# Four score banks, gathers three turns apart and another start of the experts at a kernel's change of stage

## The chip, the cores and the metric

One core of one Trainium2 chip runs the whole program. The metric is device time in microseconds of one execution. Three runs of the kernel before took 1683.93, 1685.1 and 1688.63 us; the median is 1685.1 us.

## The reference, cut to what matters

Sixteen rows of 512 tokens, 128 features wide, pass through six residual blocks:

```python
x = x + 0.5 * ffn0(layernorm(x))      # 128 -> 64 features, each through a small relu net, -> 128
x = x + attn0(layernorm(x))           # 16 heads of 8, 4 key heads, rotary positions, causal softmax
x = x + 0.5 * ffn0(layernorm(x))
x = x + 0.5 * moe(layernorm(x))       # 8 experts, 128 -> 512 -> 128
x = x + attn1(layernorm(x))           # a gated linear recurrence along the tokens
x = x + 0.5 * moe(layernorm(x))

def moe(x):                           # each expert chooses its 128 best tokens of a row
    probs = softmax(einsum('ntd,ed->nte', x, gate_w))
    g, m = top_k(probs.transpose(0, 2, 1), 128)
    h = einsum('nekf,efd->nekd', gelu(einsum('nekd,edf->nekf', x[batch, m], w1)), w2)
    return zeros.at[batch, m].add(g[..., None] * h)
```

## The kernel before

**Two parts.** First the rows go one after another through the small network and the attention, several rows in flight at different steps. Then come the experts: 256 jobs (2 expert blocks, 16 rows, 8 experts), with the recurrence of the fifth block between the two. Line numbers are those of the kernel before.

**Turns.** PE, ACT, DVE and POOL get a hand-made order. The steps are Python generators, and one turn (`turn`, L1104) advances each by one `yield`: first `flush` (L259) issues the copies left over from the last turn (`later`), then come `urgent` ones and `sides`, in list order. What is issued first stands first in its engine's queue, and each queue is in order. `need` (L221) holds a step back while the turn's budget for an engine is used up, as long as `paced` is set. `hurry` is false in the attention part and set at L1164.

**The last row's attention.** Row b has four head groups r of four heads. `weights` (L657) takes one entry of `BANKS` (L591, 11 entries) in a turn: score products on PE (L669) into a PSUM bank, the exponential on ACT (L672) into the tile `pt`, and a causal mask on POOL (L674). These exponentials are the "numerators" of the change's title. The bank comes from the pool `stp` with two buffers (L111), so the products of one turn wait for the exponential two turns before. The pool `scp` (L110), also two buffers, holds the scores from which `maxima` (L597) takes the row maxima of the next row; during the last row (b = 15) there is no next row. After a head group, `outputs` (L680) multiplies `pt` with the values into `ps_av` (L692), ACT copies that to `oT` (L696), PE transposes it (`ps_oq`, L704), and DVE divides by the sums into `y` (L708, L709) and appends r to `st["out"]` (L715). When all four are there, `stage_out` (L718) transposes y (`yT`, L721), multiplies (`ps_o`, L724), and runs the row through the second small network (`kan`, L329) and the gate (`gated`, L738). The norms in these use two POOL steps (L293, L294) between DVE steps. While the last row's attention runs, row 14 is in `stage_out` and `kan`.

**Gathers.** `fetch` (L850) gathers an expert's 128 token rows from DRAM with an indirect DMA that POOL issues (`xg`, L859), up to 16 ahead of what is transposed. It starts once the first head group's queries are done with (`taken`), as xg takes their place.

**Experts.** `dispatch` (L868) transposes gathered rows in pairs (`ps_x`, L883) and copies them to `xin` (L885, on ACT or DVE). `experts` (L891) takes three turns to a job: `ps_h` (L935) and Gelu (L937); `ps_y` (L950) and its scaling (L953); and for half the jobs products with a selection matrix into `acc` (L968), for the others an accumulating indirect DMA (L982). `ps_h` uses the banks of `scp`, `ps_y` those of `stp`. `experts` begins with two POOL steps (L908, L910). `routing` (L752) finds the top tokens on DVE, for eight rows at a time; `gated` counts scored rows for it. A job's gathers need that token list (`routed`).

**The end of the attention part** (L1164 to L1174):

```python
hurry[0], paced[0] = True, False
while len(sts[B - 1]["out"]) < NR:
    turn()
sides.append(stage_out(B - 1, sts[B - 1]))
sides.append(recurrences())
main = experts()
```

`experts` appends `dispatch` to the side tasks when it is first advanced (L925).

Of the kernel before, what the change touches and what calls it, by code (L numbers as in the profile page):

```python
# [8 lines left out]
F32 = mybir.dt.float32  # L9
# [7 lines left out]
P = 128  # L17
S = 512
# [7 lines left out]
NR = 4  # L26
# [20 lines left out]
def tile_macaron(  # L47
# [10 lines left out]
    B = x_in.shape[0]  # L58
# [40 lines left out]
    with ExitStack() as ph:  # L99
# [10 lines left out]
        scp = ph.enter_context(tc.tile_pool(name="p1_sc", bufs=2, space=PSUM))  # L110
        stp = ph.enter_context(tc.tile_pool(name="p1_st", bufs=2, space=PSUM))  # L111
# [78 lines left out]
        def packed(b):  # L190
            return [QP[(NR * b + r) % NQP] for r in range(NR)], KP[b % NKP]
# [29 lines left out]
        def need(**work):  # L221
            while paced[0] and any(w > room[e] for e, w in work.items()):
                yield
            for e, w in work.items():
                room[e] -= w

        def take(**work):

            for e, w in work.items():
                room[e] -= w  # L230
# [10 lines left out]
        held, kan_held, kans, hurry = [0], [0], [2 * B], [False]  # L241

        def bank(shape, dtype, name, work=0.0):


            while held[0] == 2 or (paced[0] and work > room["pe"]):
                yield
            room["pe"] -= work
            held[0] += 1
            return mm.tile(shape, dtype, name=name, tag="mm")  # L250

        def freed():
            held[0] -= 1
# [5 lines left out]
        def flush():  # L259
            for emit in later:  # L260
                emit()
            later.clear()
# [319 lines left out]
        def stage_in(b, st):  # L582
            late = b in through
            yield from kan_in(b)
            for _ in range(LATE if late and b > 2 else 0):
# [5 lines left out]
        BANKS = [(3, (0,)), (3, (1,)), (3, (2,)), (3, (3,)), (2, (0,)), (2, (1,)), (2, (2,)), (2, (3,)),  # L591
                 (1, (0, 1)), (1, (2, 3)), (0, (0, 1, 2, 3))]

        def in_bank(ps, gs):
            return ps.rearrange("p (u w) -> p u w", w=S // len(gs))
# [61 lines left out]
        def weights(b, st):  # L657

            qp, kp = packed(b)
            st["pt"] = {}  # L660
            for r in range(NR):
                pt = ptp.tile([P, NG, 1280], F32, name="pt")
                st["pt"][r] = pt
                for c, gs in BANKS:
                    c = NT - 1 - c
                    n = S - c * P
                    v = in_bank(stp.tile([P, S], F32, name="ps_st"), gs)
                    for u, g in enumerate(gs):
                        nc.tensor.matmul(v[:, u, 0:n], lhsT=kp[ROWS, r, bass.ts(c, P)],  # L669
                                         rhs=qp[r][ROWS, g, c * P : S], start=True, stop=True)  # L670
                    o = pt[:, gs[0] : gs[0] + len(gs), OFF[c] : OFF[c] + n]
                    nc.scalar.activation(o, v[:, :, 0:n], AF.Exp, scale=HD ** -0.5)  # L672
                    dg = o[:, :, 0:P]
                    nc.gpsimd.affine_select(out=dg, in_=dg, compare_op=ALU.is_ge, fill=0.0, base=0,  # L674
                                            pattern=[[0, len(gs)], [1, P]], channel_multiplier=-1)
                    if c == NT - 1:
                        taken[0] = NR * b + r + 1
                    yield

        def outputs(b, st, r):  # L680

            pt, va, y = st["pt"].pop(r), st["va"], st["y"]
            yield
            po = avp.tile([P, S], F32, name="ps_av")
            for c in range(NT):
                if c == 1:
                    yield
                if c < 2:
                    yield from need(pe=1.0 if c == 0 else 1.4)
                n = S - c * P  # L690
                for g in range(NG):
                    nc.tensor.matmul(po[32 * g : 32 * g + 32, c * P : S], lhsT=va[:, c, r, :],  # L692
                                     rhs=pt[:, g, OFF[c] : OFF[c] + n], start=(c == 0), stop=(c == NT - 1))
                if c == NT - 1:
                    oT = w2p.tile([P, NT, P], F32, name="oT")
                    later.append(lambda: nc.scalar.copy(oT.rearrange("p c q -> p (c q)"), po))  # L696
                if c in (0, NT - 1):
                    yield
            take(act=0.6)
            yield  # L700
            yield
            pq = yield from bank([P, NT, NG, 32], F32, "ps_oq", 0.5)
            for c in range(NT):
                nc.tensor.transpose(pq[:, c, :, :].rearrange("p r w -> p (r w)"), oT[:, c, :], ident)  # L704
            rd = small.tile([P, NT, NG, 1], F32, name="rden")

            def divide():
                nc.vector.reciprocal(rd, pq[:, :, :, HD : HD + 1])  # L708
                nc.vector.tensor_mul(y[:, :, r, :, :], pq[:, :, :, 0:HD], rd.to_broadcast([P, NT, NG, HD]))  # L709

            later.append(divide)
            yield
            take(dve=0.55)
            freed()
            st["out"].append(r)  # L715
            yield
# [131 lines left out]
        begun, fetched, moved = [0], [0], [0]  # L848

        def fetch():  # L850


            for i, (k, b, e) in enumerate(order):
                g, n = b // GB, (b % GB) * E + e
                while (k, g) not in routed or i >= moved[0] + 2 * E or taken[0] < NR * (B - 1) + min(i // E, 1) + 1:
                    yield
                if i in (0, E):
                    xgs.append(qkp.tile([CAP, E, D], F32, name=f"xg{i}", tag=f"qp{final[i // E]}"))
                nc.gpsimd.indirect_dma_start(  # L859
                    out=xgs[i // E % 2][:, i % E, :], out_offset=None, in_=xnd[b],  # L860
                    in_offset=bass.IndirectOffsetOnAxis(ap=tokI[g][:, n : n + 1], axis=0),
                )
                fetched[0] += 1

                for _ in range(3 if fetched[0] > moved[0] + 4 else 1):
                    yield

        def dispatch():  # L868
            while taken[0] < NR * B:
                yield  # L870
            for i in range(0, len(order), 2):
                while i + 1 >= fetched[0] or i > begun[0] + AHEAD:
                    yield
                if i in (0, E):
                    xins.append(qkp.tile([D, E, CAP], F32, name=f"xin{i}", tag=f"qp{final[2 + i // E]}"))

                own = kans[0] == 0
                if own:
                    ps = kap.tile([D, 2, CAP], F32, name="ps_x", tag="ps_kg")
                else:  # L880
                    ps = yield from bank([D, 2, CAP], F32, "ps_x")
                for j in range(2):
                    nc.tensor.transpose(ps[:, j, :], xgs[i // E % 2][:, i % E + j, :], ident)  # L883
                copy = nc.vector.tensor_copy if i % 4 else nc.scalar.copy
                later.append(lambda copy=copy, i=i, ps=ps: copy(xins[i // E % 2][:, i % E : i % E + 2, :], ps))  # L885
                yield
                if not own:
                    freed()
                moved[0] += 2

        def experts():  # L891
# [30 lines left out]
                else:  # L922
                    nc.sync.dma_start(out=out[b], in_=sums.pop((k, b)))

            sides.append(dispatch())  # L925
            while begun[0] < len(order) or any(line):
                now = None
                if begun[0] < moved[0]:
                    i = begun[0]
                    now = order[i] + (i % 4,)  # L930
                    k, b, e, u = now
# [11 lines left out]
                if line[1]:  # L943
                    k, b, e, u = line[1]
# [9 lines left out]
                if prod[2]:  # L954
                    v = line[2][-1]
# [5 lines left out]
                if prod[3]:  # L961
                    k, b, e, u = line[3]
# [16 lines left out]
                if line[2] and not prod[2]:  # L979
                    k, b, e, u = line[2]  # L980
                    g, n = b // GB, (b % GB) * E + e
                    nc.gpsimd.indirect_dma_start(  # L982
                        out=sums[k, b], out_offset=bass.IndirectOffsetOnAxis(ap=tokI[g][:, n : n + 1], axis=0),
# [104 lines left out]
        def recurrences():  # L1088
            while scored[0] < B:
                yield  # L1090
            for pair in range(B // 2):
                while done[0] < 2 * pair + 2:
                    yield
                yield from recurrence(pair)
# [4 lines left out]
        sts = [dict() for _ in range(B)]  # L1099
        urgent = []  # L1100
        sides = []
        TURNS = NR * len(BANKS)

        def turn():  # L1104
            flush()
            urgent[:] = [g for g in urgent if step(g)]
            sides[:] = [g for g in sides if step(g)]
            refill()
# [53 lines left out]
            if b >= 0 and b + 2 < B:  # L1162
                finish(ins[b + 2])
        hurry[0], paced[0] = True, False  # L1164
        while len(sts[B - 1]["out"]) < NR:
            turn()
        sides.append(stage_out(B - 1, sts[B - 1]))
        sides.append(recurrences())
        main = experts()
        working = True  # L1170
        while working or sides:
# [58 lines left out]
```

## Time and profile before

| what | value |
|---|---|
| median of three runs | 1685.1 us |
| profiled execution, its own time | 1679.07 us |
| its span on the profile | 1677.3 us |
| PE / DVE / ACT / POOL busy | 94% / 67% / 60% / 61% of the span |
| first gather, first ps_x, first ps_h | 919.02, 962.2, 964.73 us |
| gathers | 256, median 969 ns on POOL |

All times in what follows are microseconds from the start of the span of this one execution; 1.8 us of its time lie outside the span. "Busy" counts an engine's instructions from start to end; a PE that runs at a lower granted clock is busy for longer with the same work. A row of the timeline gives start, duration, engine, line, operation, output and input, and in brackets the idle time just before it with what ended that. A row of the waits gives the waiting instruction, what it waited for, the total in us, how often, and the longest. A row of the table by stretches gives start and end, length, and for each engine its busy time and number of instructions, then PE's granted clock as a share of full rate, the share of the DMA engines in use and GB/s.

### The profile page before, as it was taken

Reading aid. Unit: us, or ns where it says so; the run is one execution under the profiler, and the core shown is the slowest. Engines: PE = TensorE matmul, PEld = TensorE weight load, DVE = VectorE, ACT = ScalarE, POOL = GpSimd, SP = SyncE. Lnnn points to the kernel's source line nnn. Section 1 sums busy time; section 2 is a strip of 40 time slices with the busy share of each in tenths; the row PEclk is TensorE's granted clock in tenths of the full one; section 3 lists DMA queues with packets and bytes.
Section 4 is the critical chain, followed back from the end, with each engine's and each line's share of the span. In section 5 each row is a group of like instructions: output and inputs, shape, how many; then the busy total and the mean of one; then the engine's idle time right before and its main releaser. Section 6 shows DMA issues by size and latency. Waiting matters only on the chain.

```text
span 1677.3 us, 35404 instructions
## 1 busy us (share of the span) xinstructions
PE 1573.0 (94%) x12943; PEld 1093.7 (65%) x12943; DVE 1124.6 (67%) x3606; ACT 1002.3 (60%) x2000; POOL 1023.6 (61%) x1486
## 2 busy tenths in 40 slices
PE   5689999999999999999999799999999999999998
PEld 2234444444444544455444399888998889999998
DVE  6578878888888888888986146843469544672222
ACT  3446677787777877777777565444443434444454
POOL 2635557556665556565634757657766668667774
PEclk9779999999999999999999799999999999999999
DMA  4210111111101110111122114223323233333333
GB/s 123 67 63 26 56 50 40 33 42 57 53 30 40 49 57 23 40 52 56 35 81 62 30 40 78 58 52 76 64 59 64 58 61 73 67 64 75 70 77 58
DMA packets 103093, 94.87 MB, mean 57 GB/s; under 512 B 13197, under 2 KB 91478, under 8 KB 102678
## 3 DMA queue, kind: packets, MB, share of 16 engines
q1 hardware_dynamic: 76060, 67.65, 13.1%
q0 software_dynamic: 26048, 24.93, 9.4%
q8 instruction: 102, 1.67, 0.4%
q14 instruction: 73, 0.60, 0.1%
q10 hardware_dynamic: 810, 0.02, 0.0%
HBM read 59.00 MB, written 37.49 MB: 58 GB/s over the span
## 4 chain that ended last, share of the span: by engine, by line
PE 71%; DVE 19%; ACT 5%; issue 3%; POOL 2%; DMA 1%; DVEq 0%; SPq 0%; POOLq 0%; ACTq 0%
PE ps_h L935 12%; PE ps_y L950 11%; PE ps_av L692 7%; PE ps_st L669 6%; PE ps_sc L611 5%; DVE below L616 5%; PE acc L968 4%; PE ps_kg L365 4%; PE ps_s L338 3%; PE ps_t L318 3%; DVE ln_st L287 2%; ACT pt L672 2%; PE ps_ko L386 2%; PE ps_h L1076 2%; PE ps_h L1075 1%
## 5 line engine op out<-in xcount | busy, mean ns | idle before, releaser
L674 POOL TENSOR_SCALAR_AFFINE_SELECT pt<-pt 128x128 f32<-128x128 f32 (+2 forms) x704 | 252.7, 366 | 331.4 <-ACT pt L672 326.6
L672 ACT ACTIVATE pt<-ps_st 128x512 f32<-128x512 f32 (+1 forms) x704 | 378.8, 563 | 99.8 <-PE ps_st L669 94.0
L616 DVE CUSTOM_DVE_ANT_0 below<-ps_sc,causal 128x512 bf16<-128x512 f32 (+1 forms) x512 | 315.0, 615 | 80.1 <-PE ps_sc L611 64.8
L937 ACT ACTIVATE mo<-ps_h 128x512 f32<-128x512 f32 x256 | 152.8, 597 | 290.4 <-PE ps_h L935 288.5
L859 POOL DMA_INDIRECT xg<-xnd,tokI x256 | 252.3, 986 | 80.9 <-issue 45.0
L669 PE MATMUL ps_st<-qp,kp 99*128 99x512 bf16 (+3 forms) x1024 | 258.5, 305 | 21.7 <-ACT pt L672 20.8
L935 PE MATMUL ps_h<-xin,mw 128*128 128x128 f32 x2048 | 278.3, 279 | 0.0
L950 PE MATMUL ps_y<-mw,mo 128*128 128x128 f32 x2048 | 271.1, 275 | 0.4 <-DVE mo L959 0.4
L611 PE MATMUL ps_sc<-kp,qp 72*128 72x512 bf16 (+3 forms) x1024 | 259.6, 305 | 11.6 <-DVE maxs L616 6.6
L935 PEld LDWEIGHTS ps_h<-xin,mw 128*128 128x128 f32 x2048 | 249.7, 192 | 6.1 <-issue 3.2
L950 PEld LDWEIGHTS ps_y<-mw,mo 128*128 128x128 f32 x2048 | 249.1, 192 | 1.5 <-DVE mo L959 1.3
L982 POOL DMA_INDIRECT sum<-ye,tokI x124 | 201.4, 1624 | 63.4 <-ACT ye L953 22.7
L669 PEld LDWEIGHTS <-kp 99*128 99x128 bf16 x1024 | 95.1, 100 | 181.7 <-issue 164.4
L371 ACT ACTIVATE kan_h<-kan_s,rbias,kw 128x512 f32<-128x512 f32 x256 | 205.7, 812 | 3.8 <-PE ps_kg L365 3.8
L692 PE MATMUL ps_av<-pt,va 128*32 128x512 f32 (+3 forms) x2048 | 165.5, 441 | 0.0
L621 DVE TENSOR_REDUCE maxs<-ps_sc 128x2 f32<-128x512 f32 (+1 forms) x192 | 130.1, 685 | 34.9 <-PE ps_sc L611 34.4
L611 PEld LDWEIGHTS <-qp 72*128 72x128 bf16 x1024 | 96.2, 99 | 79.8 <-issue 57.2
L956 DVE TENSOR_TENSOR mo<-mo 128x128 bf16<-128x128 f32 x132 | 38.2, 290 | 129.4 <-ACT mo L941 129.1
L692 PEld LDWEIGHTS ps_av<-pt,va 128*32 128x32 f32 x2048 | 53.7, 109 | 94.9 <-issue 44.1
L968 PE MATMUL acc<-mo 128*128 128x128 bf16 x1584 | 111.3, 219 | 3.1 <-DVE mo L956 3.0
L968 PEld LDWEIGHTS <-mo 128*128 128x128 bf16 x1584 | 98.6, 98 | 19.9 <-issue 18.6
L294 POOL TENSOR_TENSOR ln_rstd<-ln_rstd,mhalf 128x4 f32<-128x4 f32 x96 | 101.1, 1053 | 8.0
(197 smaller groups left out, 2362.2 us busy)
## 6 DMA issues: line engine op xcount, KB each, us to landing
qp<-qs SPq DMA_DIRECT2D x64, 288.0 KB
xnd<-kan_x SPq DMA_DIRECT2D x32, 256.0 KB
sum<-x SPq DMA_DIRECT2D x31, 256.0 KB
qs<-qpart SPq DMA_DIRECT2D x48, 128.0 KB
kp<-ks SPq DMA_DIRECT2D x48, 96.0 KB
x<-in_L_attn_x_dram SPq DMA_DIRECT2D x16, 256.0 KB
mw<-in_L_ffn_w_dram SPq DMA_DIRECT2D x16, 256.0 KB
xg<-xnd,tokI POOLq DMA_INDIRECT x256
```

The costliest lines, as they stand in the source:

```text
L371: nc.scalar.activation(h, sk[half], AF.Relu, bias=rbias[:, half, v : v + 1], scale=kw1[:, half, v : v + 1])
L611: nc.tensor.matmul(v[:, u, 0:n], lhsT=qp[r][0 : 9 * HD, g, bass.ts(c, P)], rhs=kp[0 : 9 * HD, r, 0:n], start=alone, stop=(u == len(gs) - 1 ...
L616: nc.vector.tensor_tensor_reduce(below[:, 0:n], v[:, 0, 0:n], causal[:, S - n : S], 1.0, LOWEST, ALU.add, ALU.max, accum_out=maxs[:, c, h ...
L669: nc.tensor.matmul(v[:, u, 0:n], lhsT=kp[ROWS, r, bass.ts(c, P)], rhs=qp[r][ROWS, g, c * P : S], start=True, stop=True)
L672: nc.scalar.activation(o, v[:, :, 0:n], AF.Exp, scale=HD ** -0.5)
L674: nc.gpsimd.affine_select(out=dg, in_=dg, compare_op=ALU.is_ge, fill=0.0, base=0, pattern=[[0, len(gs)], [1, P]], channel_multiplier=-1)
L692: nc.tensor.matmul(po[32 * g : 32 * g + 32, c * P : S], lhsT=va[:, c, r, :], rhs=pt[:, g, OFF[c] : OFF[c] + n], start=(c == 0), stop=(c == ...
L859: nc.gpsimd.indirect_dma_start(out=xgs[i // E % 2][:, i % E, :], out_offset=None, in_=xnd[b], in_offset=bass.IndirectOffsetOnAxis(ap=tokI[ ...
L935: nc.tensor.matmul(pst[:, f, :], lhsT=mw1[e][:, bass.ts(f, P)], rhs=xins[i // E % 2][:, i % E, :], start=True, stop=True)
L950: nc.tensor.matmul(py, lhsT=hs[u][:, f, :], rhs=mw2[e][:, f, :], start=(f == 0), stop=(f == NF - 1))
L968: nc.tensor.matmul(acc[:, c, :], lhsT=sels[u][:, bass.ts(c, P)], rhs=yes[u][:, w, :], start=(e == 0 and c == 0 and w == 0), stop=(e == las ...
L982: nc.gpsimd.indirect_dma_start(out=sums[k, b], out_offset=bass.IndirectOffsetOnAxis(ap=tokI[g][:, n : n + 1], axis=0), in_=ye[:, b % 2 * ( ...
```

## The change

It has four parts. In the last row, every second entry of `BANKS` (counted over the four head groups) takes its bank from `scp` instead of `stp`; the new tile is called `ps_sl`. `outputs` notes in `st["read"]` how many head groups have had their last product into ps_av issued. `fetch` waits three turns after a gather, unless `hurry` is set and fewer than five gathers are ahead; before, it waited one turn whenever fewer than five were ahead. At the end of the attention part `dispatch` joins the side tasks at once, ahead of `stage_out` of the last row and `recurrences`, and the loop ends when the last head group's products have been issued, rather than when its y has been.

```diff
@@ weights @@
-                for c, gs in BANKS:
+                for i, (c, gs) in enumerate(BANKS):
                     c = NT - 1 - c
                     n = S - c * P
-                    v = in_bank(stp.tile([P, S], F32, name="ps_st"), gs)
+
+                    if b == B - 1 and (r * len(BANKS) + i) % 2:
+                        ps = scp.tile([P, S], F32, name="ps_sl", tag="ps_sc")
+                    else:
+                        ps = stp.tile([P, S], F32, name="ps_st")
+                    v = in_bank(ps, gs)
@@ outputs @@
                 if c == NT - 1:
+                    st["read"] = r + 1
@@ fetch @@
-                for _ in range(3 if fetched[0] > moved[0] + 4 else 1):
+                for _ in range(1 if hurry[0] and fetched[0] <= moved[0] + 4 else 3):
                     yield
@@ experts @@
-            sides.append(dispatch())
             while begun[0] < len(order) or any(line):
@@ tile_macaron @@
         hurry[0], paced[0] = True, False
-        while len(sts[B - 1]["out"]) < NR:
-            turn()
+        sides.append(dispatch())
         sides.append(stage_out(B - 1, sts[B - 1]))
         sides.append(recurrences())
+        while sts[B - 1]["read"] < NR:
+            turn()
         main = experts()
```

## The prediction

> **What bounds the kernel now.** I read the page first: engine shares, the 40 slices, and the chain that ended last.
>
> ```profile
> PE 1573.0 (94%) x12943; PEld 1093.7 (65%) x12943; DVE 1124.6 (67%) x3606; ACT 1002.3 (60%) x2000; POOL 1023.6 (61%) x1486
> ...
> PE   5689999999999999999999799999999999999998
> ...
> PEclk9779999999999999999999799999999999999999
> ```
>
> TensorE is busy nearly throughout and carries 71% of the chain, so only time in which it idles or runs at a low clock can be won. After the first slices there is one such place: slice 23 of 40, from about 922 to 964 us, with a 7 in both rows. There the last row's attention ends and the experts begin, which is where the change works. I then cut that stretch where the output products (ps_av) of each head group of the last row begin, with the experts' steady part behind it.
>
> ```profile
> core 0: us, PE busy (x) PEld busy (x) DVE busy (x) ACT busy (x) POOL busy (x), PEclk, DMA share, GB/s
> ...
> 907.50:918.60 11.10, 9.54 (x90) 5.68 (x88) 5.40 (x22) 8.21 (x17) 5.44 (x14) 1.00 0.45 125
> 918.60:933.20 14.60, 10.13 (x67) 5.26 (x66) 3.13 (x13) 7.11 (x14) 12.95 (x22) 0.79 0.13 32
> 933.20:945.80 12.60, 10.10 (x63) 3.59 (x62) 0.55 (x2) 10.02 (x19) 8.33 (x15) 0.77 0.07 18
> 945.80:955.70 9.90, 8.69 (x67) 3.64 (x66) 0.55 (x2) 7.86 (x15) 5.99 (x15) 0.91 0.08 20
> 955.70:970.20 14.50, 11.68 (x101) 9.54 (x101) 6.83 (x28) 5.27 (x9) 7.77 (x12) 0.88 0.15 42
> 970.20:1677.30 707.10, 697.30 (x6553) 653.75 (x6551) 364.01 (x1206) 327.19 (x773) 480.46 (x430) 1.00 0.33 65
> ```
>
> Each stretch has another limit. In the first (918.6 to 933.2, "A") POOL is busy 12.95 of 14.60 us. In the second ("B") ACT is the fullest at full rate, 10.02 of 12.60; PE's 10.10 is at a clock of 0.77. In the third ("C") it is PE, 8.69 of 9.90. In the tail ("T") nothing is full. The timeline of A shows why POOL counts:
>
> ```profile
> 923.62 0.94 POOL L859 DMA_INDIRECT xg<-xnd,tokI  x1 [0.17 <-issue]
> ...
> 925.05 0.94 POOL L859 DMA_INDIRECT xg<-xnd,tokI  x1 [0.17 <-issue]
> 926.03 0.25 POOL L293 TENSOR_SCALAR ln_rstd<-ln_mv 128x4 f32<-128x4 f32 x1
> 926.36 1.05 POOL L294 TENSOR_TENSOR ln_rstd<-ln_rstd,mhalf 128x4 f32<-128x4 f32 x1
> ...
> 927.44 0.78 DVE L308 TENSOR_TENSOR kan_x<-x,ln_rstd 128x512 f32<-128x512 f32 x1 [6.18 <-POOL ln_rstd L294]
> ...
> 928.27 1.12 PE L318 MATMUL ps_t<-ident,kan_x 128*128 128x128 f32 x4 [3.48 <-DVE kan_x L308]
> ```
>
> Row 14's norm has its sums on DVE at 921.3, but its two POOL steps stand behind five gathers (919.02, 920.76, 922.20, 923.62, 925.05); PE waits 3.48 us in its queue for what follows. The waits of PE from 917 to 970 us name the rest:
>
> ```profile
> PE ps_st L669 <- ACT pt L672: 4.9, 9, 0.7
> PE ps_t L318 <- DVE kan_x L308: 3.5, 1, 3.5
> PE ps_t L318 <- DVE y L709: 1.9, 1, 1.9
> PE ps_oq L704 <- ACT oT L696: 0.7, 1, 0.7
> ```
>
> The first is the two-bank rotation, the last two belong to T.
>
> **The gathers.** Nothing is added: 256 gathers as before. In the built order of POOL, two of them now stand ahead of row 14's two norm steps, where five did. Each costs 0.94 plus about 0.17 of issue, so 3 x 1.11 = 3.3 us leave A. If POOL sets A, the wait for its last mask before the next ps_av (932.98) moves by that much. After it, POOL needs 4 gathers (4.5), 11 masks (8 x 0.30, 2 x 0.41, 0.64) and the norm (1.3): 9.6 us from 919.0, so A could shrink by at most 5.0. I take 3.4, as PE then reaches the transposition a little before its input still, and its clock is better. The gathers' cost does not vanish: 11 instead of 16 have been issued when the first transposition of gathered rows (ps_x) is queued. The missing five come later on POOL, which is busy 480 of 707 us in the experts; what hides them is that PE sets the pace there.
>
> **Four banks.** The rotation's 4.9 us in 9 waits are PE's, not the path's: behind a waiting score product on PE stand ps_av, the FFN products and the transpositions, and ACT waits for those in turn (the waits of ACT: oT 4.0 us, the exponentials pt 4.8 in all). No instruction is added: of the last row's 64 score products 32 (22 of its 44 banks) write a bank of the other pool, whose readers (the maxima) are finished by 908.4; its next users are the experts' ps_h, after the last of them. With four banks PE may be four turns ahead of ACT, so ACT has about 2 us of exponentials (0.60 each) queued while PE does a ps_av lump of 1.50. The floors are the fullest engine: B cannot be below 10.0 (gain at most 2.5), C not below 8.7 (at most 1.2). I take half of each, 1.3 and 0.6, because from 937.5 to 945.0 ACT runs without a break already. Row 15's first head group (907.5 to 918.6) has PE at 9.54 of 11.10 and depends on the same row-14 work; I count nothing there.
>
> Here a rule speaks against the change. Cut into pieces of 3.4 us, the granted clock falls to 0.50 in three spells (927.0 to 933.9, 940.7 to 947.5, 961.2 to 964.6). The one at 940.7 follows 3.4 us in which PE was 1.85 us busy and never waited over 0.8; spells with 2.84 of 3.40 or more busy stayed at 1.00. The Trainium skill ("TensorE: Matmul & The Clock Gate", section "A second HAM failure mode: psum-queue depth-cycling") says that a product loop which cycles through PSUM banks idles so finely that the clock swings between half and full; more banks to cycle would then change nothing, B and C would keep their length, and the sum would lose 1.9. By the row, what counts is the busy share. B would have about 8.2 us of full-rate products in 11.3, 73%, between the 54% that fell and the 84% that held. I take one cold spell left in the loop, mostly under ACT; that is why B gets half only.
>
> **Experts from "read".** In the built order, three ps_x pairs now stand between the last ps_av products, and the first two ps_h ahead of and behind ps_oq, instead of after the whole chain oT, ps_oq, y, ps_t. They fill PE's idle 0.70 (for oT), 1.87 (for y) and 0.25, and the half-rate spell from 961.2, in which 3.02 us busy were worth 1.5. T holds 11.68 - 1.5 = 10.2 us of full-rate work in 14.5, so at most 4.3. The Gelu table load (1.28 us on ACT) now comes before row 15's yT copy; PE has the second ps_h, ps_x and ps_t meanwhile, and without that cover it would cost its 1.3. I take 3.0. Moved with it: dispatch stands ahead of row 15's output stage among the side tasks and takes PSUM banks first, so row 15's scores come at expert job 20 instead of 18 (built order), its token list at job 51 instead of 49. DMAs keep their number; on SP two row stores swap places. PE's order from the k=1 jobs on is the same.
>
> **Sum.** A 3.4, B 1.3, C 0.6, T 3.0: 8.3 us off. The profiled execution (span 1677.3, its time 1679.07) would come to 1670.8; it lies 6.0 below the median of the runs, 1685.1, to which the same difference applies: 1676.8. All floors reached: 5.0 + 2.5 + 1.2 + 4.3 = 13.0, 1672.1.
>
> **Rivals.** *Cold loop* (25%): PE's clock still falls in A and B, and ACT and PE keep each other's pace. Then the gathers give 2.5 and T 1.5: 1681. For it: ACT is unbroken for 7.5 us of B. Against: the fall at 927 follows the 3.48 us wait that goes.
> *The banks do nothing, the rest works* (inside the forecast's range): 1685.1 - 6.4 = 1678.7.
> *Nothing arrives* (9%): row 14's chain is limited by ACT's own queue, and what T gains is waited for at the experts' first products: 1684.
> *Gathers become the bound* (6%, slower): with 11 instead of 16 ahead, and three turns to a gather as to an expert job, the lead stays smaller: 9 instead of 14 at the first pair, mostly 4 to 5 instead of 5 to 6 for jobs 50 to 120. Before, a pair's gathers end 8.1 to 16 us ahead of their ps_x there; the one wait (1.2 us) came where only 0.17 was left, 3.5 sufficed. One gather less takes about one job, 2.6 us. The pair of jobs 58 and 59 had 9.3 us and loses two jobs to the later token list: about 4.1 left. It decides only if POOL lags 3 us more: then some 30 pairs would each pay about 0.5, 15 us in all, against the 8.3: 1692.
>
> **How the numbers follow.** The forecast has 60%, the cold loop 25%, nothing 9%, slower gathers 6%. A measurement of this kernel tells about 0.3%, 5 us: faster is below 1680.0. Most of the forecast case and a small part of the cold loop lie there: 0.66. Within: 0.26. Slower, with small unseen losses beside the last rival: 0.08. The range runs from all floors (1672.0) over the cold loop, with 2.5 us of spread, to 1683.5.
>
> **What would show it.** Right: the norm's POOL steps near 922.7 and PE's wait for kan_x under 1 us; A about 11 us long; waits of PE for ACT on score products under 2 us in total; first ps_h about 948 to 950 on the span, before ps_oq; at most one spell at 0.50 in the loop; the experts from the fifth ps_h on shifted as a block. Wrong: ps_x waiting for DMA by more than a few us, a longer experts' part than 707 us, or B still 12.6 with PE at half clock.

## The result and the profile after

The changed kernel takes 1676.4 us (median of 5 runs, 1675.01 to 1678.27); the kernel before, timed with it, takes 1684.19 (5 runs, 1682.11 to 1688.63). The ratio is 0.9951, with a 95% interval of 0.9934 to 0.9968, so 5.4 to 11.1 us are gone. The forecast was 1676.8. Its sum, 8.3 us, meets the measured difference of 7.8; the terms of the sum do not all meet theirs, as follows.

The profiled execution after took 1675.11 us (span 1673.4). The first lines of its page answer to those shown of before:

```profile
PE 1578.0 (94%) x12943; PEld 1095.9 (65%) x12943; DVE 1123.0 (67%) x3606; ACT 1001.9 (60%) x2000; POOL 1023.5 (61%) x1486
...
PE   5689999999999999999999899999999999999998
...
PEclk9779989999999999999999999999999999999999
```

The number of instructions is the same on every engine. In slice 23 of 40 the 7 of the clock is now a 9, and the 7 of PE an 8. The same cuts as before, at the starts of the last row's ps_av groups, in the table by stretches:

```profile
914.40:924.60 10.20, 9.39 (x89) 5.57 (x86) 5.31 (x22) 7.55 (x17) 5.06 (x13) 1.00 0.48 136
924.60:933.80 9.20, 8.06 (x68) 4.15 (x68) 3.15 (x13) 6.66 (x14) 8.31 (x16) 1.00 0.09 21
933.80:945.00 11.20, 9.17 (x63) 3.28 (x62) 0.55 (x2) 10.05 (x20) 9.71 (x18) 1.00 0.09 26
945.00:954.30 9.30, 9.03 (x69) 3.82 (x68) 0.56 (x3) 8.08 (x16) 6.82 (x16) 1.00 0.11 29
954.30:967.00 12.70, 12.13 (x117) 10.13 (x117) 7.22 (x30) 7.16 (x14) 8.73 (x12) 1.00 0.20 53
967.00:1673.40 706.40, 696.37 (x6534) 651.97 (x6533) 362.25 (x1204) 325.53 (x768) 482.93 (x432) 1.00 0.33 65
```

A went from 14.6 to 9.2, and POOL's 12.95 in it to 8.31. The clock was 0.79, 0.77, 0.91 and 0.88 from A to T and is 1.00 in every row. T is shorter and nearly full: PE 12.13 of 12.70. How row 14's norm got on its way, from the timeline:

```profile
927.70 0.97 POOL L865 DMA_INDIRECT xg<-xnd,tokI  x1 [0.17 <-issue]
928.95 0.24 POOL L293 TENSOR_SCALAR ln_rstd<-ln_mv 128x4 f32<-128x4 f32 x1
...
930.36 0.78 DVE L308 TENSOR_TENSOR kan_x<-x,ln_rstd 128x512 f32<-128x512 f32 x1 [3.07 <-POOL ln_rstd L294]
931.19 0.66 PE L318 MATMUL ps_t<-ident,kan_x 128*128 128x128 f32 x4 [1.01 <-DVE kan_x L308]
```

DVE's wait for the norm's POOL steps fell from 6.18 to 3.07, PE's in turn from 3.48 to 1.01, and its transposition takes 0.66 us at full rate instead of 1.12. The waits of PE from 914 to 977 us:

```profile
PE ps_t L318 <- DVE y L715: 1.3, 2, 0.7
PE ps_t L318 <- DVE kan_x L308: 1.0, 1, 1.0
PE ps_sl L674 <- ACT pt L677: 0.7, 1, 0.7
...
PE ps_st L674 <- ACT pt L677: 0.6, 1, 0.6
```

The score products wait 1.3 us in 2 waits, where they waited 5.5 in 10 over the same part (from 907 us; 4.9 in 9 from 917).

**Reading two spans against each other.** The last row's first score product starts at 907.53 us before and at 914.45 after, 6.92 later, although no engine's order ahead of it has changed. PE's half-rate time ahead of that mark was 54.6 us before and 68.3 after. When each kernel was profiled again, the marks were at 910.63 (before) and 913.65 (after). So the spans differ by 3.9 us only, while the changed stretch itself, from that mark to the first ps_h of expert job 48, went from 186.51 to 175.48: 11.0 us less. From there the parts are alike, 255.20 and 255.35 to job 128, 328.11 in both from there to the end. In what follows I therefore compare lengths from that mark. The repeats show how well these stand: 186.57 for before and 175.50 for after.

### The profile page after: what moved, and what is told of

Same layout as the page of the kernel before. It is cut to its first block, busy times and chain, and to the rows that moved or that the text cites. A ratio compares the mean times of both kernels' runs of the same rounds, so it can differ in the third digit from the quotient of the medians.

```text
span 1673.4 us, 35410 instructions
## 1 busy us (share of the span) xinstructions
PE 1578.0 (94%) x12943; PEld 1095.9 (65%) x12943; DVE 1123.0 (67%) x3606; ACT 1001.9 (60%) x2000; POOL 1023.5 (61%) x1486
## 4 chain that ended last, share of the span: by engine, by line
PE 72%; DVE 18%; ACT 4%; issue 3%; POOL 3%; DMA 0%; DVEq 0%; POOLq 0%; ACTq 0%
PE ps_h L940 12%; PE ps_y L955 11%; PE ps_av L697 7%; PE ps_st L674 6%; PE ps_sc L611 6%; DVE below L616 5%; PE acc L973 5%; PE ps_kg L365 3%; PE ps_s L338 3%; PE ps_t L318 3%; ACT pt L677 2%; DVE ln_st L287 2%; PE ps_h L1081 2%; PE ps_ko L386 2%; PE ps_h L1080 1%
## 5 line engine op out<-in xcount | busy, mean ns | idle before, releaser
L677 ACT ACTIVATE pt<-ps_st 128x512 f32<-128x512 f32 x682 | 368.3, 563 | 97.1 <-PE ps_st L674 91.4
L674 PE MATMUL ps_st<-qp,kp 99*128 99x512 bf16 x992 | 251.8, 305 | 16.7 <-ACT pt L677 16.2
```

## The experiments

Each length in the table runs from the mark to the first ps_av group of the last head groups ("0"), then from group to group (A, B, C), and from the last group to job 4 (T). "Half rate" gives where, in us behind the mark, the granted clock was 0.50 up to job 48, and in brackets for how long.

```
kernel               gathers   0      A      B      C      T    mark to  half rate
                     ahead*                                      job 4
before                  5    11.04  14.64  12.60   9.93  16.53   64.74   19.5 (6.8) 33.2 (6.8) 53.7 (3.4)
after                   2    10.14   9.21  11.21   9.32  12.69   52.57   none
e1 banks only           5    10.14  14.15  11.22   9.91  16.62   62.04   20.3 (3.4) 51.1 (3.4)
e2 pace only            2    11.04   9.46  12.30   9.49  18.37   60.66   30.2 (3.4) 47.3 (6.8)
e3 start only           5    11.04  14.66  12.60  10.93  12.24   61.47   19.5 (6.8) 33.2 (6.8) 166.3 (13.7)
e4 gather every turn    5    11.05  14.65  14.02   9.23  15.78   64.73   19.5 (6.8) 33.2 (6.8) 74.2 (3.4)
e5 after, two banks     2    11.04   9.46  12.29   9.77  12.93   55.49   30.3 (3.4) 163.5 (10.2)
e6 after, old pace      5    10.14  14.62  12.59  10.12  12.24   59.71   19.6 (6.8) 33.3 (3.4) 70.8 (3.4) 166.4 (13.7)
e7 after, old start     2    10.26   9.22  11.21   9.10  17.71   57.50   47.3 (3.4)
e8 after, six turns     1    10.14   8.34  11.21   9.32  16.42   55.43   47.7 (3.4) 160.4 (13.7)
e9 after, more          1    10.14   8.37  10.96   9.07  12.70   51.24   none
e10 after again         2    10.14   9.22  11.21   9.32  12.70   52.59   none
e11 before again        5    11.04  14.64  12.63   9.95  16.54   64.80   19.6 (6.8) 33.2 (6.8) 53.7 (3.4)
e12 after, late dispatch 2   10.14   9.22  11.21   9.10  14.88   54.55   none
* gathers ahead of row 14's norm steps in POOL's built order
```

The measured medians (this kernel, before on the same chip, ratio with its 95% interval):

```
e1   1744.05  1743.21  0.9990 [0.9967, 1.0013]      e7   1726.76  1746.44  0.9911 [0.9881, 0.9940]
e2   1744.26  1743.21  0.9982 [0.9954, 1.0011]      e8   1738.36  1746.44  0.9967 [0.9949, 0.9985]
e3   1743.45  1743.21  0.9985 [0.9961, 1.0008]      e9   1669.75  1683.74  0.9909 [0.9886, 0.9932]
e4   1742.69  1743.21  1.0004 [0.9979, 1.0029]      e10  1674.46  1683.74  0.9936 [0.9912, 0.9960]
e5   1732.10  1746.44  0.9922 [0.9900, 0.9945]      e11  1681.81  1683.74  0.9990 [0.9972, 1.0007]
e6   1742.16  1746.44  0.9982 [0.9961, 1.0002]      e12  1672.46  1683.74  0.9934 [0.9907, 0.9960]
```

The runs of e1 to e4 were on one chip and those of e5 to e8 on another, on which the kernel before takes some 60 us more than in the first comparison and in that of e9 to e12. That time lies in the experts' part and is told at the end; up to the tail, the lengths of unchanged parts agree with those of the first comparison to 0.02 us, with one exception in e3. So for e1 to e8 the verdicts rest on the lengths of one profile each, and the ratio is a second witness only: the intervals of e1 to e4 and of e6 all hold 1.

My theory was that three separate gains add up: the gathers ahead of the norm set A, the banks set B and C, the early start sets T. The rivals were that the clock does it, and that one part does nothing.

**e1, the banks alone.**

```diff
-                for c, gs in BANKS:
+                for i, (c, gs) in enumerate(BANKS):
...
-                    v = in_bank(stp.tile([P, S], F32, name="ps_st"), gs)
+                    if b == B - 1 and (r * len(BANKS) + i) % 2:
+                        ps = scp.tile([P, S], F32, name="ps_sl", tag="ps_sc")
+                    else:
+                        ps = stp.tile([P, S], F32, name="ps_st")
+                    v = in_bank(ps, gs)
```

> The kernel before with the four banks alone. The stretch from the first score product of the last row to the first ps_h of expert job 48 took 186.5 us before and 175.5 after. Theory of separate causes: five gathers still stand ahead of row 14's norm on POOL, so A loses only the bank waits (about 1 us), B loses 1.4 and C 0.6, the tail nothing: stretch near 183.5, time about 3 us below before (ratio 0.998). Rival, the clock does it: the 3.5 us wait of PE in A stays, the clock falls behind it as before, and B and C keep their 12.6 and 9.9: stretch 186, ratio 1.000.

A and B of e1, from the table by stretches:

```profile
921.80:935.90 14.10, 9.41 (x67) 5.21 (x66) 3.16 (x13) 6.89 (x15) 12.63 (x21) 0.88 0.09 28
935.90:947.20 11.30, 9.27 (x67) 3.34 (x69) 0.55 (x2) 10.00 (x19) 8.21 (x16) 1.00 0.09 25
```

Banks take 0.9 us from the first head group and 1.4 from B. A stays at 14.15, with POOL at 12.63 of it: the banks leave A's cause where it was, and the 0.5 us that it lost belong to a shorter half-rate spell (see "Why the prediction was right"). C does not gain from banks alone (9.91).

**e2, the pace of the gathers alone.**

```diff
-                for _ in range(3 if fetched[0] > moved[0] + 4 else 1):
+                for _ in range(1 if hurry[0] and fetched[0] <= moved[0] + 4 else 3):
```

> The kernel before with the three-turn spacing of the gathers alone. Separate causes: two gathers instead of five stand ahead of the norm, A goes from 14.6 to about 11, B and C stay at 12.6 and 9.9 because two banks still tie PE to ACT, tail unchanged: stretch near 182.5, ratio 0.998. Rival, the clock does it: without the long wait no spell of 0.50 follows in A or B, and B and C shrink as they did after (11.2, 9.3) though the banks are two: stretch near 179.5, ratio 0.996.

A falls to 9.46 with two banks as well. B stays at 12.30, and nine score products still wait for ACT, 5.5 us in all. The tail gets longer, 18.37 against 16.53. The trace shows where a part of that comes from: two of the gathers that the new pace puts off (950.38 and 951.63) now stand ahead of the POOL steps of row 14's next norm (952.61), and DVE waits 2.30 us for these, against 1.50 before, where one gather stood there and POOL still waited for DVE. The last y, and PE's ps_t of it, stand behind this norm: ps_t starts 6.39 us behind the last group's first ps_av, before 5.59. Besides, the half-rate spell in the tail is 6.8 us long instead of 3.4.

**e3, the start alone.**

```diff
+                    st["read"] = r + 1
...
-            sides.append(dispatch())
...
-        while len(sts[B - 1]["out"]) < NR:
-            turn()
+        sides.append(dispatch())
         sides.append(stage_out(B - 1, sts[B - 1]))
         sides.append(recurrences())
+        while sts[B - 1]["read"] < NR:
+            turn()
```

> The kernel before with dispatch and the experts started early alone. Separate causes: A, B and C as before (14.6, 12.6, 9.9), only the tail gains, 2.6 us by job 48: stretch near 184, ratio 0.9985. Rival: the tail's gain in the changed kernel came only because PE arrived there at full rate; then the stretch is 186 and the spell of 0.50 behind 961 stays.

T falls by 4.3, and C rises by 1.0. Of this, 0.3 is the first pair of gathered rows, whose transposition now stands in C (958.23), and 0.8 a longer wait of a score product for ACT (1.32 us, before 0.55), for which the edit gives no reason. Net 3.3.

**e4, the opposite of the new pace.** All gathers of the last row one turn apart:

```diff
-                for _ in range(3 if fetched[0] > moved[0] + 4 else 1):
+                for _ in range(3 if hurry[0] and fetched[0] > moved[0] + 4 else 1):
```

> The kernel before with a gather in every turn of the last row until 16 are issued (before: five close together, then three turns apart). The suspected cost of A nearly doubled: about four more gathers of 1.1 us fall between the first one and the last mask that ps_av waits for. If POOL sets A: A grows by 3 to 4.5 us to about 18, B and C lose their gathers and shrink a little (0 to 1), stretch 188 to 190, ratio 1.001 to 1.002. If A is set by PE's or ACT's order instead: A within 1 us of 14.6.

A and B of e4, table by stretches:

```profile
924.90:939.60 14.70, 10.22 (x70) 5.30 (x69) 3.20 (x13) 7.18 (x15) 13.05 (x22) 0.79 0.12 36
939.60:953.60 14.00, 10.30 (x63) 3.65 (x62) 0.55 (x2) 10.02 (x19) 12.59 (x21) 0.74 0.13 39
```

I had expected A at 18, and it stayed at 14.65. The edit differs from before only after the fifth gather, and the norm stands behind five in both, so A should have stayed. The added gathers show where they stand: POOL's 8.33 in B became 12.59, and B 14.02. C and T were shorter by 1.5 together, so the whole to job 4 is the same, 64.73. For A, what counts is how many gathers stand in front of the waited-for POOL step; denser gathers behind it cost A nothing, though they lengthen B.

**e5, e6, e7: the change without one of its parts.** e5 keeps `stp` for all banks, e6 the old condition in `fetch`, e7 the old start of the experts (each the reverse of the diff of e1, e2 and e3).

> The changed kernel with the four banks undone. After: A 9.2, B 11.2, C 9.3, stretch to job 48 175.5 us. Separate causes: PE is tied to ACT's exponentials again, A about 10.2, B 12.6, C 9.9, stretch near 178.5, time about 3 us above after. Rival, the clock does it: no long wait, no spell of 0.50, all as after within 1 us.

> The changed kernel with the old spacing of the gathers. Separate causes: five gathers ahead of row 14's norm again, A back to 13 or more (the bank waits stay away), with a wait of PE for kan_x of 3 us or more and perhaps a spell of 0.50 behind it; B and C 11.2 and 9.3 if the banks carry them; stretch near 179.5, time 3.5 to 4 us above after. Rival: with PE four banks ahead the norm's delay is covered; stretch within 1 us of 175.5.

> The changed kernel with the old start of dispatch and experts. Separate causes: A, B, C as after; the tail gets its waits back (0.7 for oT, 1.9 for y) and perhaps a spell of 0.50: stretch 178 to 179, time 2.6 us above after. Rival: the tail's waits were a consequence of the slow loop; stretch within 1 us of 175.5.

Without the banks, 2.9 us of the 12.2 to job 4 are missing; without the pace 7.1, without the start 4.9. Alone, the parts gave 2.7, 4.1 and 3.3. So pace and start need each other: with the old start and the new pace T is 18.37 (e2) and 17.71 (e7, where PE waits 1.9 us for oT and 1.5 for y), with the old start and the old pace 16.53 (before) and 16.62 (e1), and with the new start 12.24 to 12.93 (e3, e5, e6 and after). In e7, as in e2, and in the changed kernel too (954.81 and 956.06, the norm at 957.03), two gathers stand right ahead of row 14's next norm; in the changed kernel PE has the experts' first products meanwhile.

e6 also holds a warning. Up to T it is the program of e1, with four banks and the old pace. Yet B is 11.22 in e1 and here

```profile
939.90:952.50 12.60, 11.20 (x65) 3.48 (x64) 0.55 (x2) 10.02 (x19) 8.12 (x17) 0.80 0.08 23
```

with PE's clock at 0.80 for 1.00 and PE busy 11.20 for 9.27. A half-rate spell in B takes the banks' whole gain away. With four banks and the new pace no spell fell in A, B or C in any of the six profiles (after, e7, e8, e9, e10, e12), with two banks there was one in B every time.

**e8, gathers six turns apart in the last row.**

```diff
-                for _ in range(1 if hurry[0] and fetched[0] <= moved[0] + 4 else 3):
+                for _ in range((1 if fetched[0] <= moved[0] + 4 else 3) if hurry[0] else 6):
```

> The changed kernel with six turns between gathers in the last row (one gather ahead of row 14's norm, six instead of eleven issued at the first ps_x). POOL no longer holds A back after the change, so A within 0.5 of 9.2. It tests the rival in the prediction, that a small lead makes the gathers the bound: if a lead of about four suffices, the stretch is within 1 us of 175.5 and PE's waits for gathered rows stay under 2 us in all; if it does not, the first 20 jobs wait, and the stretch is 178 or more.

One gather ahead of the norm gives A = 8.34, 0.9 less than two. But only 6 gathers have been issued at the first ps_x, instead of 11, and the waits of PE from 920 to 985 us now hold

```profile
PE ps_x L889 <- DMA xg<-xnd,tokI: 2.6, 1, 2.6
```

T is 16.42. This is the rival in which the gathers become the bound: it exists. Ten gathers are enough (e9, with T at 12.70), so its point lies between a lead of 6 and one of 10.

**e9, an attempt at a better version.** One gather ahead of the norm, three turns after that; and in the last row the copies to oT and, in the same way, of the small network's first products (`kan`) move from ACT to DVE:

```diff
-                for _ in range(1 if hurry[0] and fetched[0] <= moved[0] + 4 else 3):
+                for _ in range((1 if fetched[0] <= moved[0] + 4 else 3) if hurry[0] else 6 if fetched[0] == 1 else 3):
...
-                    later.append(lambda: nc.scalar.copy(oT.rearrange("p c q -> p (c q)"), po))
+                    copy = nc.vector.tensor_copy if b == B - 1 else nc.scalar.copy
+                    later.append(lambda: copy(oT.rearrange("p c q -> p (c q)"), po))
...
```

> The changed kernel with two further edits: six turns instead of three between the first and the second gather, so that one gather stands ahead of row 14's norm; and the last row's copies out of PSUM that ACT does (oT, and the next small network's input kan_s) on DVE, which is 0.55 us busy in all of B. Theory: A goes from 9.2 to 8.3 as with six turns throughout, B, whose fullest engine was ACT at 10.06 of 11.21, to about 10.3, C to 9.0, and the tail stays within 0.7 of 12.7 to job 4, since ten gathers are out by then: about 2 us below the changed kernel on the same chip. Rival: B is held by the order of PE and ACT, not by ACT's work, and stays within 0.3 of 11.2.

A and B of e9, table by stretches:

```profile
923.90:932.20 8.30, 7.85 (x67) 4.11 (x66) 3.90 (x15) 6.10 (x13) 7.37 (x15) 1.00 0.06 17
932.20:943.20 11.00, 9.22 (x65) 3.31 (x64) 2.54 (x5) 8.70 (x17) 9.58 (x18) 1.00 0.09 25
```

Its median is the lowest of all, 1669.75, ratio 0.9909 to before, but the interval overlaps that of the changed kernel on the same chip (e10). What is sure is the stretch from the mark to job 48: 174.21, 1.3 us shorter than that of after. A gave 0.84 of that. In B, ACT has 1.35 us less to do (10.05 to 8.70), and B is only 0.25 shorter, where I had expected 0.9. So ACT's amount of work does not hold B once there are four banks. What does is open: no engine is full there (PE 9.22, POOL 9.58 of 11.0).

**e10 and e11, both kernels again, unchanged.**

> The changed kernel once more, on a chip of the experiments: A 9.2, B 11.2, C 9.3, to job 4 12.7 as on the first chip. If the half-rate spell near job 41, which the four kernels with the early start showed on these chips and those with the old start did not, belongs to the early start, it is here as well, and the ratio to before is 0.993 to 0.996; if it was chance, it is absent and the ratio is near 0.990.

> The kernel before once more, for its trace on a chip of the experiments: stretches up to the tail as on the first chip (A 14.6, B 12.6, C 9.9, to job 4 16.5); ratio 1.000. Its experts part says how much of the 60 us by which these chips are above the first lies there: expected nearly all.

No stretch up to job 4 moved by more than 0.03 us. e11 against before is 0.999, with 1 in the interval. The half-rate spell near job 41, which all four kernels with the new start had on the two slower chips and none of the four others, is absent in e10, so the new start alone does not bring it. The ratio, 0.9936, is nevertheless the one expected with the spell.

**e12, the new end of the loop, but dispatch where it was.**

```diff
+            sides.append(dispatch())
             while begun[0] < len(order) or any(line):
...
-        sides.append(dispatch())
```

> The changed kernel with dispatch begun only when the experts are (the loop still ends when the last products are issued). If the tail's gain comes from filling PE's waits for oT and y with the experts' first products, those now come about three turns later, behind three pairs of transpositions: to job 4 about 14 us against 12.7. If the loop's end alone matters: within 0.4 of 12.7. A, B and C as in the changed kernel.

The tail on PE, from the timelines, first after:

```profile
957.34 1.16 PE L940 MATMUL ps_h<-xin,mw 128*128 128x128 f32 x8
958.34 0.60 PE L710 MATMUL ps_oq<-ident,oT 128*128 128x128 f32 x4
...
960.62 0.63 PE L318 MATMUL ps_t<-ident,y 128*128 128x128 f32 x4 [0.57 <-DVE y L715]
```

and e12:

```profile
951.40 0.66 PE L710 MATMUL ps_oq<-ident,oT 128*128 128x128 f32 x4 [0.39 <-ACT xin L891]
...
952.11 1.06 PE L941 MATMUL ps_h<-xin,mw 128*128 128x128 f32 x8
954.56 0.63 PE L318 MATMUL ps_t<-ident,y 128*128 128x128 f32 x4 [1.40 <-DVE y L715]
```

With the late dispatch the first ps_h comes behind ps_oq, and PE waits 1.40 us for y, against 0.57. T is 14.88, nearer to the 14 expected if these first products matter than to the 12.7 expected if they do not. e7, e12 and after differ in one step each (e7 on a slower chip): the mark to job 4 goes from 57.50 to 54.55 by the loop's earlier end and to 52.57 by the earlier dispatch, so the two are worth 3.0 and 2.0 us. At job 48 the dispatch still has 1.5 (177.01 against 175.48). In the runs e12 (0.9934) and e10 (0.9936) cannot be told apart, as their intervals are 0.5% wide.

## Why the prediction was right, and where its sum was not

The forecast's mechanism arrived: no engine does less, and the time came out of PE's waits and half clock in the one slice that was named. Step by step, in us:

```
             predicted   before -> after    measured   floor given
stage 0          0        11.04 -> 10.14       0.9         -
A               3.4       14.64 ->  9.21       5.4        5.0
B               1.3       12.60 -> 11.21       1.4        2.5
C               0.6        9.93 ->  9.32       0.6        1.2
T, to job 4     3.0       16.53 -> 12.69       3.8        4.3
job 4 to 48      0       121.77 -> 122.91     -1.1         -
sum             8.3      186.51 -> 175.48     11.0       13.0
```

**The gathers** are the term that was mis-sized. The count was right: POOL had five gathers ahead of the norm, then two, and e2 and e5 show that the pace alone does it. Three of them make 3.3. The rest the prediction had put at 0.1, for "its clock is better". The chain of work before, first, shows where it was:

```profile
926.36 1.06 POOL ln_rstd L294
927.44 0.79 DVE kan_x L308
928.27 1.13 PE ps_t L318 x4
...
931.14 1.71 PE ps_s L338 x2
...
933.28 1.30 PE ps_av L692 x8
```

and the timeline after:

```profile
932.52 1.12 PE L338 MATMUL ps_s<-kan_xT,win 128*128 128x512 f32 x2
...
933.65 0.97 POOL L865 DMA_INDIRECT xg<-xnd,tokI  x1 [0.16 <-issue]
933.79 1.07 PE L697 MATMUL ps_av<-pt,va 128*32 128x512 f32 x8
...
934.62 1.24 POOL L679 TENSOR_SCALAR_AFFINE_SELECT pt<-pt 128x256 f32<-128x256 f32 x3
```

Behind the norm A runs on PE, from ps_t to the next ps_av, in both kernels with the same products. This part took 4.94 us before (928.27 to 933.21), at half rate and with one wait of 0.32, and 2.60 after (931.19 to 933.79). The part ahead of it, from A's start to this ps_t, went from 9.70 to 6.60. Where only the pace differs, the split is 3.5 and 1.7 (before to e2) and 3.6 and 1.8 (e6 to after). So the wait in POOL's queue was sized about right, and the half rate behind it, 1.7 us or more, was the missing term. e1 agrees: its shorter spell covers 3.4 us of PE's part, in e6 all 4.45 are at half rate, and half of that difference is the 0.5 by which e1's A is shorter (14.15 and 14.62).

The spell did not follow PE's wait of 3.48 us, as the prediction has it; it began inside it:

```profile
923.40:927.00 3.60, 1.28 (x8) 0.76 (x7) 0.00 (x0) 1.91 (x5) 3.13 (x6) 1.00 0.21 55
927.00:930.40 3.40, 1.97 (x10) 1.62 (x11) 1.24 (x3) 0.98 (x3) 3.21 (x7) 0.51 0.00 0
```

PE idled from 924.79 to 928.27, and the clock fell at 927.0. All six profiles with five gathers ahead have a spell here, and none of the eight with one or two. The pace takes both away at once; no run separates the wait from the spell.

The floor of 5.0 was wrong too. It took all of POOL's masks of this head group, and the one that ends at 932.98, for what the next ps_av waits for. That last mask belongs to the next group already, and after the change ps_av starts at 933.79, ahead of the last two masks of its own group (from 934.62 on), which stand behind a fourth gather. So three gathers, not four, end in A.

**Stage 0** was counted at nothing, since PE looked full in it (9.54 of 11.10). The banks gave 0.9 there in every kernel that had them but one (0.8). It is the same rotation, and a PE that is 86% busy still waited.

**B and C** came out as predicted in size, by a choice of half the floor, for a reason that holds only in part; that half was right is luck. The waits of the score products fell as named, from 4.9 to 1.3. But e6 shows that the clock decides whether it arrives, which was the cold-loop rival's case, and e9 that ACT's work is not the floor that I took it for. C's gain does not come from the banks alone (e1 9.91); 0.4 of it comes from the pace alone (e2 9.49).

**The rule on bank cycling** (the Trainium skill, "TensorE: Matmul & The Clock Gate", section "A second HAM failure mode: psum-queue depth-cycling") spoke for B and C unchanged, as the prediction read it; the page tells it of one other kernel, and that more banks would change nothing was the prediction's own step. The traces agree with the rule as far as two banks go: all six profiles with two banks have a 0.50 spell in B. The step fails at least together with the new pace: with four banks and the new pace none of the six profiles has one in A, B or C. e6, with four banks and the old pace, has one in B and e1 has none, so four banks alone do not settle it. The busy share, which the prediction took instead, was 82% in B (9.17 of 11.20), where 73% (8.2 us of full-rate products) had been worked out and one spell allowed for. None came.

**T** gave 3.8 at job 4, within the floor, and 2.7 by job 48. "Shifted as a block" was wrong: between the two 1.1 us is given back. Row 15's output steps lie two jobs later than before, as the prediction said of its scores (job 20 instead of 18), and the lengths of jobs 6 to 20 after are nearly those of jobs 4 to 18 before. PE has the same number of products between jobs 4 and 48 in both and does not idle, so the 1.1 is no wait; why the same products take longer in this order is open.

**The lucky part.** 1676.8 came from a median of 1685.1, and 8.3 off. The stretch gave 11.0, and the five-run median of before was 0.9 lower. Measured by medians the gain was 7.8 in the first comparison and 9.3 in the second (1683.74 to 1674.46); both intervals hold 11.0. The near hit of 0.4 us is closer than the terms deserved: A was 2.0 too low, and stage 0 and the part behind job 4, both put at nothing, nearly cancel.

**The rivals.** That nothing arrives fell with A. That the banks do nothing fell with e1 and e5. That the gathers become the bound did not happen with 11 ahead: PE's waits for gathered rows in the experts were 1.4 us in one wait, 1.2 before. e8 shows that 6 would have been too few, e9 that 10 suffice. The cold loop stays true as a condition on B.

## What to carry to other kernels

Count what stands ahead of a waited-for step in its engine's queue, DMA issues included, and price the wait together with the half-rate spell that comes with it: here the wait's own share was about 3.5 us and the whole 5.4. What is put off in a queue comes up again: ask which later step it will then stand ahead of. An early start of the next stage pays where its first work fills waits of the last one, and it can keep another gain whole: of the 5.2 us that the pace took from A, 4.1 were left at job 4 with the old start (e2). Compare traces from the first instruction that the change can reach: the spans differed by 3.9 us, the changed stretch by 11.0, and repeats of that stretch agreed to 0.1.

## What the runs showed of the hardware that I had not expected

**A half-rate spell without an idle window.** Before, pieces of 3.4 us in B, table by stretches:

```profile
937.30:940.70 3.40, 1.85 (x14) 1.07 (x11) 0.55 (x2) 3.22 (x7) 1.74 (x4) 1.00 0.00 0
940.70:944.10 3.40, 2.45 (x13) 1.04 (x14) 0.00 (x0) 3.40 (x7) 3.22 (x7) 0.50 0.10 29
944.10:947.50 3.40, 3.40 (x17) 0.31 (x9) 0.00 (x0) 1.54 (x3) 2.14 (x5) 0.50 0.13 31
```

In the first, PE is 54% busy at full rate and its two waits are 0.7 us at most; 6.8 us at 0.50 follow. Such spells do not repeat exactly: in A one began 19.6 us behind the mark in e6 and lasted 6.8, and in e1, the same program up to there, one began at 20.3 and lasted 3.4.

**Chips on which the same kernel is 3.5% slower.** Before took about 1684 us in the first comparison and on the chip of e9 to e12, and 1743 and 1746 on the two others. Each group of runs was on one chip at one time, so the chip and the time are not told apart. The attention part is alike. The experts' jobs 48 to 128 took 272 to 286 us there for 255 (259 in e10), and the rest 352 to 360 for 328. Between 970 and 1640 us PE, DVE and ACT idle together for 0.35 to 0.82 us at 3 to 11 moments in a profile there, at one moment on the other chips (one is in e3 near 1072 us, where the profile puts a wait of ACT, 1.37 us, and one of DVE, 3.09, down to no engine of the core). Half-rate spells of 10 to 14 us stand in the same part, 31 to 74 us at half rate behind the mark in a profile, against 2 to 19 on the other chips. What stops the engines, and whether that brings the spells, was not settled. It also blurs e3, e5, e6 and e8, which had such a spell near job 41 (160 to 166 us behind the mark), so that their times by job 48 no longer show the tail's gain; that is why those are read to job 4.
